# A graph layer's gather: 74 single rows per step instead of 40, in three list loads, with the list at partition 64

## The chip, the cores and the metric

The kernel runs on one core of one Trainium2 chip. The metric is the device time of one execution in microseconds. Before the change it is 15,322.12 us, the median of three runs (15,321.51 to 15,322.25).

## What is computed

One layer of a graph network with 50,000 nodes of 128 features and 1,650,000 edges, which are sorted by destination. Cut to what matters:

```python
Xs = X[src]
m_data = Xs @ W_data.T + b_data
m_ctrl = Xs @ W_control.T + b_control
msg = jnp.where((edge_types == 0)[:, None], m_data, m_ctrl)
agg = jax.ops.segment_sum(msg, dst, num_segments=X.shape[0])
x = _layernorm(x + relu(agg + (X @ W_self.T + b_self)))
```

For each edge the feature row of its source (512 bytes) has to be fetched, the rows are summed by destination and by edge type, and the sums go through the weights afterwards, since the products are linear.

## The kernel before

**Blocks and steps.** The sorted edges are cut into blocks, and a block into two steps (Q = 2). A step holds 12 chunks of 128 edges (R = 12), F = 42 fillers and S = 40 single rows, that is 1,618 edges; a block holds 3,236. The first block and the last hold chunks alone. This makes NBLK = 510 blocks.

**Three ways for an edge.** The rows of a chunk are fetched by one indirect DMA that POOL issues (`gathers`, L477): 128 rows into one column of a tile `y`, 24 such gathers per block, in four passes of six. There are ten tiles (SLOTS), so POOL may run some two and a half blocks ahead of the matmuls. The fillers take the place of edges in a chunk whose source is their own destination, since such rows need not be fetched; DVE puts them in (`fill`, L316 to L338). The single rows (`single_rows`, L437) go without POOL: SP and ACT issue one plain DMA of 512 bytes per row (L451), whose source address lies in a register. TURNS = (20, 20) says how many of a step's rows go by SP and by ACT.

**The list of single rows.** `load_edges` (L163) brings the row numbers of ten blocks into one partition (`one_g`); `offsets` (L430) has DVE multiply those of one block by 512 and write `at_x` (L435), 80 numbers in the order: SP's 40, then ACT's 40. Each queue reads its part of `at_x` into registers with a load (L446, TENSOR_LOAD in the profile), LOADS = 2 times per block, 20 numbers each, and issues 20 row fetches after each load. SP has another such load, L400, which reads the window starts of five blocks from the list `base_i`; DVE has one of one number per step, L509; and at the end each engine reads one number, L943.

**What PE does.** For each chunk a matmul (L496) with a one-hot matrix `oh` sums the rows by destination and type into `acc`. Once per step a further matmul (L502) adds the single rows. Ahead of it PE waits until all rows of the block have landed (`rows_fetched`, L456, wait at L460).

**What sets the order.** All is written out by hand, without a scheduler: each engine and queue runs its instructions in the order of the main loop (L614). In the turn of block b, the engines work like this:
- SP loads `xT` of block b+3 (L406), once in ten blocks the next group's edges, then the two parts of the single rows of block b+2, then stores the output of block b-1 (L563).
- ACT issues part 0 of the rows of block b+2, takes the square root for block b-1 (`root`, L551), which waits for DVE's moments (L546), and issues part 1.
- DVE finishes block b-1 (L541 to L546), builds the one-hot matrix and the counts of block b+2 (L412, L420), takes ACT's root (L557) and writes the output (L559), fills block b+5, and writes the row list of block b+3 (L435).
- A row tile `yx` has four buffers; the first fetch of a block waits until PE has used up the block four before.

Of the kernel before, what the change touches and what calls it, by code (L numbers as in the profile page):

```python
# [15 lines left out]
I32 = mybir.dt.int32  # L16
# [21 lines left out]
PASS = 6  # L38
B = 112
C = R * Q  # L40
F = 42
TURNS = (20, 20)
S = sum(TURNS)
LOADS = 2
X = Q * S
R1 = R + 1
C1 = Q * R1
# [2 lines left out]
CE = Q * SIZE  # L50
BE = CE + Q * F + X
NBLK = 2 + (E - CE) // BE
# [4 lines left out]
GB = 10  # L57
GROUPS = -(-NBLK // GB)
GC = GB * C1
AHEAD = 2  # L60
# [21 lines left out]
def plain(b):  # L82

    return b == 0 or b >= NBLK - 1
# [6 lines left out]
def straight(ctx, tc, c, x, x_t, src_t, dst_t, etype_t, src_f, dst_f, etype_f, src_x, dst_first, first_p, out):  # L91
# [17 lines left out]
    eds = ctx.enter_context(tc.tile_pool(name="eds", bufs=2))  # L109
# [3 lines left out]
    stp = ctx.enter_context(tc.tile_pool(name="stp", bufs=3))  # L113
# [13 lines left out]
                   allow_small_or_imprecise_dtypes=True)  # L127
    FILL = Q * F + C1
    small = keep_ps.tile([P, 2 * W + F + 2 * FILL + 2], F32, name="small")
    num_ps, rank_no_ps = small[:, :2 * W], small[:, 2 * W:2 * W + F]  # L130
    lists = [small[:, 2 * W + F + i * FILL:][:, :FILL] for i in range(2)]
    sums_at = [small[:Q * F, 2 * W + F + 2 * FILL + i:][:, :1] for i in range(2)]

# [27 lines left out]
    one_g = {}  # L161

    def load_edges(g):  # L163
        t = eds.tile([1, GB * X], I32, name="one_g")
        nc.sync.dma_start(t, src_x[None, g * GB * X:(g + 1) * GB * X])
        one_g[g] = t
        loads[g] = {}
        for name, a in (("s", src_t), ("d", dst_t), ("t", etype_t)):
            t = eds.tile([P, GB, C1], I32, name=name, bufs=1)
            nc.sync.dma_start(t.rearrange("p b c -> p (b c)"), a[:, g * GC:(g + 1) * GC])  # L170
            loads[g][name] = t
        for name, a in (("sf", src_f), ("df", dst_f), ("tf", etype_f)):
            t = eds.tile([GS, F], I32, name=name, bufs=1)
            nc.sync.dma_start(t, a[g * GS:(g + 1) * GS, :])
            loads[g][name] = t


    load_edges(0)
    BL = TBL
    first_i = keep.tile([P, BL, Q], I32, name="first_i")  # L180
# [211 lines left out]
    bys, pcs, zs, pls, bases, ats, ys = {}, {}, {}, {}, {}, {}, {}  # L392
# [23 lines left out]
    def counts(b):  # L416

        cnt = ohp.tile([P, Q, 2 * W], BF16, name="cnt")
        with nc.allow_low_precision(reason="whole numbers up to R1"):
            nc.vector.tensor_reduce(cnt, ohs[b].rearrange("p (q r) w -> p q w r", r=R1), AX.X, ALU.add)  # L420
        cnts[b] = cnt
# [8 lines left out]
    def offsets(b):  # L430

        if not plain(b):
            g, i = divmod(b, GB)
            ats[b] = stp.tile([1, X], I32, name="at_x", bufs=AHEAD + 2)
            nc.vector.tensor_scalar(ats[b], one_g[g][:, i * X:(i + 1) * X], float(ROW), None, op0=ALU.mult)  # L435

    def single_rows(b, part):  # L437

        if part == 0:
            ys[b] = stp.tile([S, Q, D], F32, name="yx", bufs=ROW_SLOTS)  # L440
        both = []
        for j, (eng, dma) in enumerate(((SP, nc.sync), (ACT, nc.scalar))):
            n = Q * TURNS[j]
            k0, k1 = part * n // LOADS, (part + 1) * n // LOADS
            at = Q * sum(TURNS[:j])
            _, rows = nc.values_load_multi_w_load_instructions(ats[b][0:1, at + k0:at + k1], engines=[eng], **RANGE)  # L446
            both.append([(dma, fetched[j][b % ROW_SLOTS], *divmod(k0 + k, TURNS[j]), sum(TURNS[:j]), row)
                         for k, row in enumerate(rows)])
        for pair in zip_longest(*both):
            for dma, sem, q, k, at, row in filter(None, pair):  # L450
                copy = dma.dma_start(ys[b][at + k:at + k + 1, q, :].bitcast(U8), x_bytes[:, bass.ds(row, ROW)])  # L451
                copy.then_inc(sem, 16)
                tc.no_tile_sem_insts.add(copy.ins.name)
                tc.add_to_no_dep_group(f"single{b}", copy.ins)

    def rows_fetched(b):  # L456

        times = len(range(b % ROW_SLOTS or ROW_SLOTS, b + 1, ROW_SLOTS))
        for j in range(2):
            wait = nc.tensor.wait_ge(fetched[j][b % ROW_SLOTS], 16 * Q * TURNS[j] * times)  # L460
        tc.declare_fence(wait.ins, group=f"single{b}")
# [132 lines left out]
    for b in range(1, AHEAD + 1):  # L594
        offsets(b)
# [7 lines left out]
    for b in range(1, RAHEAD):  # L603
# [3 lines left out]
        if b < AHEAD:  # L607
            onehot(b)
            counts(b)
            for part in range(LOADS):  # L610
                single_rows(b, part)
        if b == 1:
            clear_sums()
    for b in range(NBLK + 1):  # L614
# [5 lines left out]
        if i == 0 and g + 1 < GROUPS:  # L620
            load_edges(g + 1)
# [9 lines left out]
        for q, (step, ks) in enumerate(passes_of(b)):  # L631
# [26 lines left out]
            if q == 3:  # L658
                left_out_matrix(b + RAHEAD)
                offsets(b + AHEAD + 1)  # L660
            if q < LOADS and not plain(b + AHEAD):
                single_rows(b + AHEAD, q)
# [338 lines left out]
```

## Time and profile before

| what | value |
|---|---|
| runs | 15,321.51 to 15,322.25 us, median 15,322.12 |
| profiled execution | 15,323.45 us, its span 15,321.7 us |
| mean granted TensorE clock | 0.535 |
| DMA | mean 61 GB/s, 939.07 MB in 649,293 packets |
| share of 16 DMA engines: POOL's queue q0, q1, ACT's queue q10 | 20.9%, 2.9%, 0.3% |
| instructions | 197,234 |

The profile's first part gives each engine's busy time. Issuing a DMA, loading a register and waiting are not counted as busy there, so a queue that only issues looks idle; its instructions are seen in the views by source line, which give the number, the least, median and largest duration in ns, and the first and last start in us. A line of the waits names who waited, for whom, the sum in us, how often, and the longest; "issue" means that the engine waited for nothing that the profile shows. A line of the costliest groups ends with the busy time in us, the mean of one in ns, and the idle time just before them.

### The profile page before, as it was taken

Reading aid. Unit: us, or ns where it says so; the run is one execution under the profiler, and the core shown is the slowest. Engines: PE = TensorE matmul, PEld = TensorE weight load, DVE = VectorE, ACT = ScalarE, POOL = GpSimd, SP = SyncE. Lnnn points to the kernel's source line nnn. Section 1 sums busy time; section 2 is a strip of 40 time slices with the busy share of each in tenths; the row PEclk is TensorE's granted clock in tenths of the full one; section 3 lists DMA queues with packets and bytes.
Section 4 is the critical chain, followed back from the end, with each engine's and each line's share of the span. In section 5 each row is a group of like instructions: output and inputs, shape, how many; then the busy total and the mean of one; then the engine's idle time right before and its main releaser. Section 6 shows DMA issues by size and latency. Waiting matters only on the chain. (4 is left out here: it accounts for less than half of the span.)

```text
span 15321.7 us, 197234 instructions
## 1 busy us (share of the span) xinstructions
PE 8296.6 (54%) x35844; PEld 7096.5 (46%) x35845; DVE 10904.6 (71%) x13994; ACT 153.6 (1%) x516; POOL 11565.0 (75%) x12250
## 2 busy tenths in 40 slices
PE   3555555555555555555555555555555555555555
PEld 3444444444444444444444444444444444444444
DVE  8777777777777777777777777777777777777775
ACT  0000000000000000000000000000000000000000
POOL 7777777777777777777777777777777777777777
PEclk7555555555555555555555555555555555555555
DMA  2222222222222222222222222222222222222222
GB/s 65 62 61 62 61 62 61 62 62 61 62 61 62 61 62 61 62 61 62 62 60 62 61 62 61 62 62 61 61 62 62 61 62 61 62 61 62 62 61 56
DMA packets 649293, 939.07 MB, mean 61 GB/s; under 512 B 327756, under 2 KB 445487, under 8 KB 648034
## 3 DMA queue, kind: packets, MB, share of 16 engines
q0 software_dynamic: 391680, 802.93, 20.9%
q1 hardware_dynamic: 215276, 112.76, 2.9%
q10 hardware_dynamic: 41078, 10.68, 0.3%
q14 instruction: 968, 7.93, 0.2%
q8 instruction: 291, 4.77, 0.1%
HBM read 895.92 MB, written 29.42 MB: 60 GB/s over the span
## 5 line engine op out<-in xcount | busy, mean ns | idle before, releaser
L477 POOL DMA_INDIRECT y<-in_x,idx x12216 | 11540.9, 945 | 3733.3 <-issue 3552.2
L496 PE MATMUL acc<-oh,y 128*128 128x120 f32 x24480 | 5867.6, 429 | 5768.3 <-PEq L484 5767.8
L496 PEld LDWEIGHTS acc<-oh,y 128*128 128x128 f32 x24480 | 5313.7, 326 | 6190.7 <-PEq L484 6178.3
L420 DVE TENSOR_REDUCE cnt<-oh 128x240 bf16<-128x3120 f32 x510 | 2959.6, 5803 | 0.1
L541 DVE COPY h<-po 112x128 f32<-112x128 f32 x510 | 148.7, 292 | 2499.1 <-PE po L535 2407.5
L412 DVE TENSOR_TENSOR oh<-col,small 128x3120 f32<-128x3120 f32 x510 | 1719.5, 3372 | 0.0
L512 DVE TENSOR_TENSOR sums<-acc,sums 128x180 f32 x1020 | 352.2, 345 | 1393.1 <-PE acc L505 1236.0
L338 DVE TENSOR_REDUCE by<-old 128x84 bf16<-128x1092 f32 x508 | 1078.5, 2123 | 17.6
L502 PE MATMUL acc<-oh,yx 40*128 40x120 f32 x2032 | 777.4, 484 | 0.0
L345 PE MATMUL small<-ones_b,by 128*84 128x1 bf16 x508 | 117.4, 231 | 1191.1 <-DVE by L338 1191.1
L319 DVE TENSOR_TENSOR m<-rk,small 128x1092 f32<-128x1092 f32 x508 | 656.4, 1292 | 17.3
L322 DVE TENSOR_TENSOR new<-m,small 128x1092 f32<-128x1092 f32 x508 | 656.2, 1292 | 17.3
L326 DVE TENSOR_REDUCE v_new<-new 128x26 f32<-128x1092 f32 x508 | 655.8, 1291 | 17.3
L345 PEld LDWEIGHTS <-by 128*84 128x84 bf16 x508 | 74.3, 146 | 1267.3 <-DVE by L338 1267.2
L335 DVE TENSOR_TENSOR old<-m,small 128x1092 f32<-128x1092 f32 x508 | 652.3, 1284 | 0.0
L502 PEld LDWEIGHTS acc<-oh,yx 40*128 40x128 f32 x2032 | 497.5, 304 | 210.0 <-issue 205.3
L535 PE MATMUL po<-wmsgT,sums 128*112 128x128 f32 x2040 | 515.1, 396 | 0.0
L535 PEld LDWEIGHTS po<-wmsgT,sums 128*112 128x112 f32 x2040 | 374.0, 253 | 108.2 <-issue 88.7
L533 PE MATMUL po<-bias,sums 3*112 3x128 f32 x1020 | 350.3, 439 | 0.0
L525 DVE TENSOR_TENSOR sums<-pl,sums 128x336 f32<-128x336 f32 x508 | 257.9, 508 | 85.2 <-DVE sums L512 84.6
L532 PE MATMUL po<-wselfT,xT 128*112 128x128 f32 x1020 | 315.5, 412 | 0.0
L551 ACT ACTIVATE sd<-mv,eps 112x1 f32<-112x1 f32 x510 | 150.4, 295 | 15051.3 <-DVE mv L546 8335.5
(118 smaller groups left out, 4174.2 us busy)
## 6 DMA issues: line engine op xcount, KB each, us to landing
yx<-in_x ACTq DMA_DIRECT2D x20320, 0.5 KB
yx<-in_x SPq DMA_DIRECT2D x20320, 0.5 KB
y<-in_x,idx POOLq DMA_INDIRECT x12216
xT<-in_x_t SPq DMA_DIRECT2D x510, 56.0 KB
out<-o SPq DMA_DIRECT2D x510, 56.0 KB
vf_all<-vd SPq DMA_DIRECT2D x51, 420.0 KB
s<-in_src_t SPq DMA_DIRECT2D x51, 130.0 KB
d<-in_dst_t SPq DMA_DIRECT2D x51, 130.0 KB
```

The source lines that it names most:

```text
L319: nc.vector.tensor_tensor(m, rk_g[g][:, i, :, None].to_broadcast([P, C1, F]), rank_no_ps[:, None, :].to_broadcast([P, C1, F]), op=ALU.is_e ...
L322: nc.vector.tensor_tensor(new.rearrange("p (q r) f -> p q r f", r=R1), m.rearrange("p (q r) f -> p q r f", r=R1), vf.rearrange("p (q f) -> ...
L326: nc.vector.tensor_reduce(v, new, AX.X, ALU.add)
L335: nc.vector.tensor_tensor(old, m, cb[:, :, None].to_broadcast([P, C1, F]), op=ALU.mult)
L338: nc.vector.tensor_reduce(by, old.rearrange("p (q r) f -> p q f r", r=R1), AX.X, ALU.add)
L412: nc.vector.tensor_tensor(oh, col_g[g][:, i, :, None].to_broadcast([P, C1, 2 * W]), num_ps[:, None, :].to_broadcast([P, C1, 2 * W]), op=AL ...
L420: nc.vector.tensor_reduce(cnt, ohs[b].rearrange("p (q r) w -> p q w r", r=R1), AX.X, ALU.add)
L477: copy = nc.gpsimd.indirect_dma_start(out=y[:r, k % PASS, :].bitcast(U8), out_offset=None, in_=x_rows, in_offset=bass.IndirectOffsetOnAxis ...
L496: nc.tensor.matmul(acc[:, :2, :].rearrange("p t w -> p (t w)"), y[:r, k % PASS, :], ohs[b][:r, column(k), :], start=k == of_step[0], stop= ...
L502: nc.tensor.matmul(acc[:, :2, :].rearrange("p t w -> p (t w)"), ys[b][:, q, :], ohs[b][:S, q * R1 + R, :], start=False, stop=True)
L512: nc.vector.tensor_tensor(part, accs.pop((b, q)), part, op=ALU.add)
L535: nc.tensor.matmul(po, a[:, t, :B], c["wmsgT"][:, t * D:(t + 1) * D], start=False, stop=t == 1)
```

## The change

Of each step 74 edges become single rows instead of 40, 36 of them SP's and 38 ACT's. A queue reads its list in three loads per block instead of two, and issues a third part of rows in the third pass of the main loop (`q < LOADS`). There are 43 fillers instead of 42. The parts are cut by `part * n // LOADS`: SP's 72 rows of a block into 24, 24, 24, at positions 0, 24 and 48 of the block's list, and ACT's 76 into 25, 25, 26, at positions 72, 97 and 122. The lists `one_g` and `at_x` become tiles of 65 partitions of which the last one alone is used, so that they lie at partition 64 instead of 0; in the bytes of a partition they take 148 numbers per block instead of 80.

```diff
-F = 42
-TURNS = (20, 20)
+F = 43
+TURNS = (36, 38)
 S = sum(TURNS)
-LOADS = 2
+LOADS = 3
+AT = 64
 X = Q * S
...
     def load_edges(g):
-        t = eds.tile([1, GB * X], I32, name="one_g")
+        t = eds.tile([AT + 1, GB * X], I32, name="one_g")[AT:, :]
         nc.sync.dma_start(t, src_x[None, g * GB * X:(g + 1) * GB * X])
...
             g, i = divmod(b, GB)
-            ats[b] = stp.tile([1, X], I32, name="at_x", bufs=AHEAD + 2)
+            ats[b] = stp.tile([AT + 1, X], I32, name="at_x", bufs=AHEAD + 2)[AT:, :]
             nc.vector.tensor_scalar(ats[b], one_g[g][:, i * X:(i + 1) * X], float(ROW), None, op0=ALU.mult)
```

The lines of the new kernel are numbered one higher from here on (L477 is L478 there).

## The prediction

> **What bounds the kernel now.** I read the page first for the busiest engine, then the waits of that engine, then the two queues that the change loads, SP and ACT. These are lines of the page: the busy shares, the costliest group, and the two kinds of row fetch among the DMA issues.
>
> ```profile
> PE 8296.6 (54%) x35844; PEld 7096.5 (46%) x35845; DVE 10904.6 (71%) x13994; ACT 153.6 (1%) x516; POOL 11565.0 (75%) x12250
> ...
> L477 POOL DMA_INDIRECT y<-in_x,idx x12216 | 11540.9, 945 | 3733.3 <-issue 3552.2
> ...
> yx<-in_x ACTq DMA_DIRECT2D x20320, 0.5 KB
> yx<-in_x SPq DMA_DIRECT2D x20320, 0.5 KB
> y<-in_x,idx POOLq DMA_INDIRECT x12216
> ```
>
> The waits of POOL over the whole span:
>
> ```profile
> POOL y L477 <- issue: 3559.2, 11667, 0.3
> POOL y L477 <- DVE h L542: 74.9, 245, 0.3
> ```
>
> POOL looks only 75% busy, but it is the bound: its idle time is 0.3 us behind each gather, "issue", with nothing to wait for. Start to start the 12,240 gathers (12,216 and 24 of the last block) lie 1,250 ns apart in the mean (median 1,249, 99% under 1,267). 12,240 x 1.2503 = 15,304 us of the 15,321.7 us span; the 18 us left are the start and the last block's tail. A block of 24 gathers takes 30.0 us, and every other engine and queue has room as long as it needs less than 30.0 us per block. DVE needs 10,904.6 / 510 = 21.4 us, PE 16.3 us.
>
> ACT is "1% busy", but issuing is not counted as busy. These views are the list loads and row fetches by source line, L446 over the whole span and L451 in one part of a block:
>
> ```profile
> L446 ACTq TENSOR_LOAD <-at_x x1016: 1411/1437/1689, 16.8 to 15202.4; - x170
> L446 SPq TENSOR_LOAD <-at_x x1016: 1197/1378/1676, 26.8 to 15191.8; - x170
> ```
>
> ```profile
> L451 ACTq DMA_DIRECT2D yx<-in_x x20: 227/228/461, 8028.1 to 8034.4; - x20
> ```
>
> A load of 20 row numbers takes 1.44 us on ACT, and 20 rows are issued from 8028.1 to 8034.4. Averaged over all parts, a part on ACT is the load, 0.16 us, a first row that takes 0.56 us until the second, 0.326 us for each later row, and 0.24 us for the last one's own issue: 8.3 us for 20 rows. Two parts, the square root and gaps are 16.7 us per block. So ACT has 13 us of room per block; SP, with 16.2 us of rows and some 1.9 us of other issues, has 12.
>
> **The change, part by part.**
>
> *Blocks and gathers (removed).* A step holds 1536 + 43 + 74 edges instead of 1536 + 42 + 40, a block 3,306 instead of 3,236. So there are 500 blocks, not 510, and the last has 5 gathers, not 24: 499 x 24 + 5 = 11,981 gathers, 259 fewer. If POOL stays the bound: 259 x 1.2503 = -324 us, 14,998 us of span. That is the most that the change can give.
>
> *Row issues (added).* Per block SP issues 72 rows instead of 40 and ACT 76, in parts of 24, 24, 24 and 25, 25, 26. ACT without its loads: 0.16 + 0.56 + 23 x 0.326 + 0.24 = 8.46 us for a part of 25, 8.79 for 26, together 25.7 us, and 0.24 us for the square root and gaps: 25.9 us of the 30.0. Rows from both queues go out side by side in the trace already, at 227 to 228 ns, so I add nothing for that.
>
> *List loads (added, the disputed price).* What is left for three loads on ACT is 30.0 - 25.9 = 4.1 us. Their price hangs on where they start. The trace has another load, L400, which takes 5 values each time from one list, at positions 0, 5, 10 and so on. Here are two of them, at 518.8 us (position 20) and at 668.6 us (position 25), and the loads of one value at the end:
>
> ```profile
> L400 SPq TENSOR_LOAD <-base_i x1: 746/746/746, 518.8 to 518.8; - x1
> ```
>
> ```profile
> L400 SPq TENSOR_LOAD <-base_i x1: 1329/1329/1329, 668.6 to 668.6; - x1
> ```
>
> ```profile
> L943 ACTq TENSOR_LOAD <-bad x1: 465/465/465, 15314.7 to 15314.7; - x1
> L943 DVEq TENSOR_LOAD <-bad x1: 308/308/308, 15315.2 to 15315.2; - x1
> L943 SPq TENSOR_LOAD <-bad x1: 473/473/473, 15316.0 to 15316.0; - x1
> ```
>
> All 26 loads that start at a multiple of 4 take 714 to 840 ns, the 76 others 1,260 to 1,386, for the same 5 values. Five reads of one value each fit the 76: 473 + 4 x 204 = 1,290. One read of four and one of one fit the 26. The 20 values of L446 start at positions 0, 20, 40 and 60, all multiples of 4: five reads, (1,437 - 465) / 4 = 243 ns for each further one on ACT, 226 on SP. So I read it thus: from a multiple of 4 on, values come four at a time; from elsewhere, one at a time. Position 15, three past a multiple, would show it if one value came singly and the rest as four: it took 1,315 ns, so it doesn't.
>
> After the change ACT's list begins at position 72 and its parts at 72, 97 and 122. The first is a multiple of 4, the other two are not. SP's parts (0, 24, 48) all are; the built program puts each list on a 16-byte boundary. ACT's reads: 25 values as 6 fours and a one, 1.44 + 2 x 0.243 = 1.92 us; 25 values singly, 0.465 + 24 s; 26 values singly, 0.465 + 25 s. s is 204 ns by SP's L400 and 243 by ACT's reads of four; I take 219, SP's single read raised as ACT's reads of four stand to SP's (243 / 226). That gives 1.92 + 5.72 + 5.94 = 13.6 us (12.9 at 204, 14.8 at 243) where 4.1 are free.
>
> One rule is to be weighed here. The Trainium skill, "Runtime: NRT & Kernel Launch", Instruction fetch mechanics, has a register load cost some 200 ns per register even in bulk. The trace has 72 ns per value in the loads of 20 and contradicts it there, and agrees in the 76 dear loads of five. By the rule ACT would need 15.2 us for loads, an estimate, and the run 20.5 ms.
>
> *Sum.* ACT needs 25.9 + 13.6 = 39.5 us per block and becomes the bound. Nothing slows it further: its list for the next block comes from DVE some 10 us after the square root that ACT itself issues between its first and second part, so DVE's answer is there 19 us early. ACT's steady work begins with block 3, at 103.5 us in the trace (blocks 1 and 2 fit before, 2 x 39.5 us from 16.8 us on), and covers 496 blocks up to 498; behind its last row lie the landing, half a block of matmuls and the last layer, some 30 us (from the last gather to the end it is 16 us now). 104 + 496 x 39.5 + 30 = 19,730 us; with unrounded terms 19,740.
>
> *SP.* 28.8 us for three parts of 24 (8.03 to 8.10 us each now, plus 4 rows and one read of four), 0.5 for xT, 0.55 for the store, 0.25 for L400 shared by five blocks, 0.4 for the group's loads, 0.2 gaps: 30.7 us. It hides behind ACT's 39.5, but not behind POOL's 30.0.
>
> *The rest, at nothing.* 43 fillers lengthen five DVE operations of 7.3 us per block by 26 / 1092, 0.17 us, and at_x from 0.18 us to about 0.25: DVE goes to 21.7 us and hides behind ACT; without cover it would cost 0.25 x 500 = 120 us. The matmul of L502 contracts 74 rows instead of 40; L496 with 128 rows takes 429 ns, L502 with 40 takes 484, so rows cost nothing. The fetches take 0.3% (ACT's queue) of the DMA engines now. Partition 64 is the one thing without a row: a load there can't be cheaper than the cheapest load shown, 0.3 us, and I know no row that makes it dearer than at 0, so the bounds are 0.3 us for each load and 243 ns for each read; I take no effect. DVE's load of one value at partition 0 (L509) has a median of 304 ns amid all traffic, and 308 at the end with the queues empty: no sign that partition 0 is crowded. The Trainium skill, "SBUF — State Buffer", Door 1, says that partitions 64 apart are served by different DMA ports, which speaks for the move; no row here shows a gain from it.
>
> **Rivals.**
> 1. *The end of the run is faster.* A read at partition 64 costs less than a third, so three loads fit into 4.1 us (at most some 60 ns per read instead of 219). Then SP's loads fall too, from 4.9 us below 2, POOL stays the bound, and the span is 14,998 us: 15,000. For it: nothing shows a read there. Against: the 304 and 308 ns above.
> 2. *Only the values up to the next multiple of 4 come singly*, so parts 2 and 3 take 10 and 8 reads: 2.65 and 2.17 us. ACT needs 32.7 us, 16,340 us. If position cost nothing at all: 1.92 + 1.92 + 2.17, 31.9 us, 15,980. Still slower, since three loads and 76 rows don't fit into 30.0. Against: position 15.
> 3. *ACT's loads just fit, and SP sets the pace* with 30.7 us: 134 + 496 x 30.7 = 15,360, no change.
> That the change doesn't do what it says is excluded: the built program has 500 blocks, 11,981 gathers, and three loads of 24 to 26 numbers per queue and block.
>
> **How the numbers follow.** The profiled execution took 15,323.45 us for a span of 15,321.7 us; the runs' median is 15,322.12, 1.3 us less, so the sum stands for both. What a measurement here can tell from no change is 0.2%. Forecast (singly read loads bind ACT): 0.80, 19,740 us, by itself 19,380 to 20,320. Rival 2: 0.07. Rival 1: 0.10. Rival 3: 0.03. The range runs from rival 2's 16,300, which also covers reads that are somewhat cheaper at partition 64, to 20,900, for reads that are some 5% dearer than the dearest row: 0.95 of the forecast and most of rival 2. Faster 0.10, same 0.03, slower 0.87.
>
> **What would show it.** Loads of ACT near 1.9, 5.7 and 5.9 us in turn, of SP near 1.6; ACT's rows without a gap from block to block; POOL's idle time put down to PE instead of issue, and PE waiting for the fetched rows (L461 in the new numbering). Loads of under 2 us at all three positions would prove me wrong in the position rule, loads of about 1 us in the partition.

## The result, and the profile after

The kernel with the change takes 19,693.32 us (median of four runs, 19,582.59 to 19,800.39) where the kernel before takes 15,321.83: the ratio is 1.285, with a 95% interval from 1.275 to 1.295. The profiled execution took 19,582.59 us, with a span of 19,580.9. The four runs lie in two pairs 1.1% apart (19,583 and 19,587; 19,800 twice), for which no run shows a cause, and the working below is held against the lower pair, where the profile and all four runs of the same kernel in experiment e5 lie (19,578 to 19,586).

Busy time, the chain of work that ended last, by engine and then by line, POOL's group, and the matmul L503, ahead of which PE waits for the fetched rows, from the page of the kernel after:

```profile
PE 5715.8 (29%) x35101; PEld 5373.9 (27%) x35102; DVE 10810.8 (55%) x13719; ACT 150.5 (1%) x506; POOL 11310.9 (58%) x11991
...
ACTq 85%; issue 13%; ACT 1%; DVE 1%; PE 0%; DMA 0%; SPq 0%; DVEq 0%
ACTq L452 52%; ACTq L447 33%; ACT sd L552 1%; DVE cnt L421 0%; PE acc L497 0%; DVE by L339 0%; ACTq L552 0%; DVE new L323 0%; DVE m L320 0%; DVE v_new L327 0%; DVE old L336 0%; DVE oh L413 0%; PE po L536 0%; DMA first_i<-in_dst_first 0%; PE po L534 0%
...
L478 POOL DMA_INDIRECT y<-in_x,idx x11976 | 11304.8, 944 | 8194.6 <-PE acc L497 4449.5
...
L503 PE MATMUL acc<-oh,yx 74*128 74x120 f32 x1992 | 457.2, 318 | 0.0
```

Every busy share has fallen, and ACT still shows 1%, because issuing is not counted as busy. The chain tells what the shares hide: 85% of the span is ACT's own queue, 52% the row fetches of L452 and 33% the list loads of L447. A third of the span goes into reading numbers out of a list. POOL does 11,976 gathers instead of 12,216, at the same duration (944 ns, before 945), but now sits idle for 8,195 us of the span.

The list loads by source line, over the whole span and then on ACT alone in one block (8000 to 8042 us; duration in ns as least/median/most):

```profile
L447 ACTq TENSOR_LOAD <-at_x x1494: 1889/5598/6038, 16.9 to 19540.5; - x187
L447 SPq TENSOR_LOAD <-at_x x1494: 1578/1677/1903, 27.1 to 19509.0; - x187
```

```profile
L447 ACTq TENSOR_LOAD <-at_x x4: 1997/5570/5858, 7999.3 to 8038.3; - x4
```

SP's loads of 24 values take 1.68 us. ACT's of 25 and 26 have a median of 5.6 us, and a least of 1.9: the three parts are three different loads. Sorted by part, their medians are 1.997 us at position 72, 5.598 at 97 and 5.842 at 122. The first reads as many values as the second and takes a third of the time.

Who waits for whom, from the waits of the whole span (total us, times, longest us):

```profile
PEld L346 <- DVE by L339: 12746.6, 498, 30.3
...
DVE rstd L558 <- ACT sd L552: 6678.0, 498, 25.2
POOL y L478 <- PE acc L497: 4449.5, 646, 11.0
POOL y L478 <- issue: 3332.9, 10915, 0.3
...
POOL y L478 <- PEq L461: 27.5, 90, 0.3
```

Read it from effect to cause: POOL (third line) waits for PE to give its buffers back, PE's weight load (first line) waits for DVE, DVE (second line) waits for ACT's square root in 498 blocks, up to 25.2 us, and the root stands in ACT's queue behind rows and loads. The last line is POOL's, 27.5 us. PE itself stood idle for 0.0 us ahead of L503 (first fence), so it hardly ever waited at L461 for fetched rows.

ACT's timeline in that block (start us, us, what):

```profile
8004.96 33.20 ACTq L452 DMA_DIRECT2D yx<-in_x  x76
8038.26 0.29 ACT L552 ACTIVATE sd<-mv,eps 112x1 f32<-112x1 f32 x1 [38.72 <-issue]
```

76 rows with two loads between them fill 33.2 us, the third load comes behind the root at 8038.3, and there is no gap. From block to block ACT's period is 39.22 us in the mean. SP, which has 24 us of rows and 5 us of loads, waits 4,438.6 us in the span for its next list from DVE: it is not what limits.

### The profile page after: what moved, and what is told of

Its sections match the earlier page's. It is cut to its first block, busy times and chain, and to the rows that moved or that the text cites. A ratio compares the mean times of both kernels' runs of the same rounds, so it can differ in the third digit from the quotient of the medians.

```text
span 19580.9 us, 261977 instructions
## 1 busy us (share of the span) xinstructions
PE 5715.8 (29%) x35101; PEld 5373.9 (27%) x35102; DVE 10810.8 (55%) x13719; ACT 150.5 (1%) x506; POOL 11310.9 (58%) x11991
## 3 DMA queue, kind: packets, MB, share of 16 engines
q0 software_dynamic: 383392, 785.90, 14.3%
## 4 chain that ended last, share of the span: by engine, by line
ACTq 85%; issue 13%; ACT 1%; DVE 1%; PE 0%; DMA 0%; SPq 0%; DVEq 0%
ACTq L452 52%; ACTq L447 33%; ACT sd L552 1%; DVE cnt L421 0%; PE acc L497 0%; DVE by L339 0%; ACTq L552 0%; DVE new L323 0%; DVE m L320 0%; DVE v_new L327 0%; DVE old L336 0%; DVE oh L413 0%; PE po L536 0%; DMA first_i<-in_dst_first 0%; PE po L534 0%
## 5 line engine op out<-in xcount | busy, mean ns | idle before, releaser
L478 POOL DMA_INDIRECT y<-in_x,idx x11976 | 11304.8, 944 | 8194.6 <-PE acc L497 4449.5
L497 PE MATMUL acc<-oh,y 128*128 128x120 f32 x23962 | 4166.1, 345 | 0.1
L497 PEld LDWEIGHTS acc<-oh,y 128*128 128x128 f32 x23962 | 3925.1, 255 | 0.3
L339 DVE TENSOR_REDUCE by<-old 128x86 bf16<-128x1118 f32 x498 | 1078.3, 2165 | 17.2
L323 DVE TENSOR_TENSOR new<-m,small 128x1118 f32<-128x1118 f32 x498 | 657.5, 1320 | 17.0
L320 DVE TENSOR_TENSOR m<-rk,small 128x1118 f32<-128x1118 f32 x498 | 657.4, 1320 | 16.9
L327 DVE TENSOR_REDUCE v_new<-new 128x26 f32<-128x1118 f32 x498 | 656.3, 1318 | 17.0
L336 DVE TENSOR_TENSOR old<-m,small 128x1118 f32<-128x1118 f32 x498 | 653.8, 1313 | 0.0
L503 PE MATMUL acc<-oh,yx 74*128 74x120 f32 x1992 | 457.2, 318 | 0.0
L503 PEld LDWEIGHTS acc<-oh,yx 74*128 74x128 f32 x1992 | 380.6, 237 | 0.0
```

What stands on the lines that cost most here:

```text
L320: nc.vector.tensor_tensor(m, rk_g[g][:, i, :, None].to_broadcast([P, C1, F]), rank_no_ps[:, None, :].to_broadcast([P, C1, F]), op=ALU.is_e ...
L323: nc.vector.tensor_tensor(new.rearrange("p (q r) f -> p q r f", r=R1), m.rearrange("p (q r) f -> p q r f", r=R1), vf.rearrange("p (q f) -> ...
L327: nc.vector.tensor_reduce(v, new, AX.X, ALU.add)
L339: nc.vector.tensor_reduce(by, old.rearrange("p (q r) f -> p q f r", r=R1), AX.X, ALU.add)
L478: copy = nc.gpsimd.indirect_dma_start(out=y[:r, k % PASS, :].bitcast(U8), out_offset=None, in_=x_rows, in_offset=bass.IndirectOffsetOnAxis ...
L497: nc.tensor.matmul(acc[:, :2, :].rearrange("p t w -> p (t w)"), y[:r, k % PASS, :], ohs[b][:r, column(k), :], start=k == of_step[0], stop= ...
```

## Experiments

**Theory**: a list load that starts at a multiple of four values (16 bytes) reads four at a time; from any other position it reads one at a time, at 0.21 us each. Two of ACT's three parts start elsewhere, ACT becomes the bound, and that is the loss. **Rivals**: the partition (64) sets the price of a read; or only the first values up to the next multiple of four come singly; or the positions don't matter for the time, because more rows lose anyhow. The runs were made in four groups, each on one chip with runs of the kernel before beside them.

One fact has to be known to read them. On the chips of two groups (e1 to e4, and e9 to e11) the kernel before takes 19,301.02 and 19,232.97 us instead of 15,322. There, instructions of SP and ACT stall while both issue rows at once; the last section has the numbers. In these groups SP or ACT is the bound in every kernel that was profiled (in e3, which is the kernel before but for the partition, SP waits for 0.2 ms of 19.3), so their times are compared only inside a group, and what I take from them are durations of loads. The groups of e5 to e8 and of e12 have 15,324.96 and 15,321.62 us for before.

### e1_fours and e6_fours_again: the same rows, cut at multiples of four

Against the kernel after. SP's parts stay 24, 24, 24; ACT's become 24, 24 and 28, at positions 72, 96 and 120.

```diff
-            k0, k1 = part * n // LOADS, (part + 1) * n // LOADS
+            k0, k1 = (p * n // LOADS // 4 * 4 for p in (part, part + 1))
```

> The changed kernel with the parts of the lists cut at multiples of four: ACT reads 24, 24 and 28 numbers from positions 72, 96 and 120 instead of 25, 25 and 26 from 72, 97 and 122; SP's parts stay. Theory (a load that starts off a multiple of four reads its numbers one by one): ACT's loads fall to about 1.75, 1.75 and 1.95 us, ACT needs 25.9 + 5.5 = 31.4 us per block and is still the bound, 134 + 496 x 31.4 = 15,700 us. Rival (76 rows and three loads are too many wherever they start) and rival (loads at partition 64 are dear): ACT's loads stay as they are, 19,600 to 19,800 us.

Measured in the first group: 25,691.69 us, 1.330 [1.3237, 1.3364] of before. ACT's loads fell to some 1.7, 1.7 and 2.0 us, as the theory says, but the time says nothing. SP's timeline in this run:

```profile
8000.36 9.06 SPq L452 DMA_DIRECT2D yx<-in_x  x11
```

Eleven rows take 9.06 us here; over the whole run a row takes SP 0.63 us in the mean instead of 0.33, so SP needs 51.3 us per block and no longer lets ACT's loads show. Inconclusive; the same kernel was run again in the second group.

> The changed kernel with the parts cut at multiples of four (ACT 24, 24, 28). Theory (single reads off a multiple of four made ACT the bound): where rows take 0.32 us, ACT's loads are 1.7, 1.7 and 2.0 us, ACT needs 25.9 + 5.4 = 31.3 us per block and SP 30.7: 134 + 496 x 31.3 = 15,700 us, that is 4.0 ms less than the changed kernel and still 2% more than before. Rival (76 rows and three loads cost as much wherever they start): 19,600 us.

Measured: 16,068.54 us, 1.0485 [1.0471, 1.0500] of before, beside 19,579.01 for the kernel after on the same chip (e5). The loads of e6:

```profile
L447 ACTq TENSOR_LOAD <-at_x x1494: 1647/1765/2243, 17.0 to 16014.8; - x187
L447 SPq TENSOR_LOAD <-at_x x1494: 1579/1677/1903, 27.4 to 16031.0; - x187
```

No load above 2.3 us is left. Nothing but the places of two cuts differs, and it is worth 19,579.01 - 16,068.54 = 3,510 us of the 4,254 us that the change costs on this chip. That refutes the rival in which the positions don't matter. It is still slower than before, and 370 us above the 15,700 that I expected. The chain, by engine and by line, and the largest waits of SP in e6 show where to look:

```profile
SPq 33%; DVE 21%; DMA 16%; issue 13%; ACTq 11%; PE 6%; DVEq 0%; ACT 0%; PEldq 0%
SPq L452 26%; DMA yx<-in_x 16%; ACTq L452 9%; SPq L447 6%; DVE cnt L421 5%; PE acc L497 3%; DVE by L339 3%; ACTq L447 2%; DVE new L323 2%; DVE m L320 2%; DVE v_new L327 2%; DVE old L336 2%; PE acc L503 1%; PE po L536 1%; PE po L534 1%
```

```profile
SPq L175 <- DMA out<-o: 514.2, 48, 12.3
SPq L447 <- DVE mv L547: 73.7, 80, 1.7
```

SP heads the chain now. Its block takes 30.69 us in the median, more than POOL's 30.0; but the mean is 32.1, because once in ten blocks, where a group's lists are loaded, it takes 46 us: L175 waits 514.2 / 48 = 10.7 us there. This is such a place:

```profile
3288.37 0.34 SPq L564 DMA_DIRECT2D out<-o  x1
...
3292.50 0.34 SPq L175 DMA_DIRECT2D df<-in_dst_f  x1
3302.97 0.28 SPq L175 DMA_DIRECT2D tf<-in_edge_type_f  x1
```

The load of tf stands still from 3292.8 to 3303.0 until a store issued at 3288.4 has landed, 14.6 us after its issue. The store is late because it queues behind rows: in the trace's packet records a row's packet begins 8.3 us after its issue here (median), 0.7 us in the kernel before and 0.64 in the kernel after, where the same rows are spread over 39 us. The store itself shows it: 105 of its 112 packets begin within 2 us of its issue, the last seven at 3300.8 us, behind rows of SP that begin one after another until then. In 475 stores of this run it is seven each time, one sixteenth, in the median 9.0 us after the issue. That would fit if the rows of a queue all went through one of the 16 DMA engines, but the records don't name the engine. The chain's "DMA yx<-in_x 16%" is time between the issue of a row and its landing.

The wait need not be all of it. Through the six blocks that lead up to such a wait, the delay of ACT's rows grows from 4.7 to 11.1 us, 1.0 us per block. So in these blocks, in which SP doesn't wait, SP and ACT issue their rows faster than the queues take them up. No run takes away the wait alone; how the last 700 us divide between the two stays open.

### e2_partition0 and e10_partition0_again: the lists back at partition 0

Against the kernel after.

```diff
-AT = 64
+AT = 0
```

> The changed kernel with the lists back at partition 0, all else as changed. Theory (position in the list decides, not the partition): loads of 2.0, 5.6 and 5.8 us on ACT as at partition 64, 19,600 to 19,800 us, the same as the changed kernel. Rival (partition 64 makes the loads dear): loads of under 2.2 us and some 15,900 us.

> The changed kernel with its lists at partition 0, where rows are issued in 0.32 us. Theory (the partition has no effect): 19,580 us, the same as the changed kernel. Rival (partition 64 makes each read dearer): ACT's loads fall below 5 us and the time with them.

Measured: 26,122.65 us, 1.3525 [1.3461, 1.3590], and 26,025.93 us, 1.3547 [1.3523, 1.3571]. Both fell on chips that stall, so the times expected were missed and the kernel has no time on another chip. The loads are answer enough. Those of e10:

```profile
L447 ACTq TENSOR_LOAD <-at_x x1494: 822/5547/6097, 16.6 to 26039.4; - x187
L447 SPq TENSOR_LOAD <-at_x x1494: 3/1675/1927, 27.4 to 26007.0; - x187
```

By part, ACT's medians are 1.99, 5.55 and 5.85 us at partition 0, and 1.997, 5.598 and 5.842 at 64.

### e3_64_alone: partition 64 without the rest

Against the kernel before; its 40 rows and two loads are kept.

```diff
-        t = eds.tile([1, GB * X], I32, name="one_g")
+        t = eds.tile([AT + 1, GB * X], I32, name="one_g")[AT:, :]
...
-            ats[b] = stp.tile([1, X], I32, name="at_x", bufs=AHEAD + 2)
+            ats[b] = stp.tile([AT + 1, X], I32, name="at_x", bufs=AHEAD + 2)[AT:, :]
```

> The kernel before with the lists at partition 64 and nothing else. Theory: loads of 20 numbers take 1.44 us on ACT and 1.2 to 1.46 on SP as at partition 0, and POOL stays the bound: 15,322 us, no change. Rival (partition 64 makes loads dear): loads of 4 us or more; ACT and SP have 12 us of room, so the time would hide it and only the loads tell.

Measured: 19,330.95 us beside 19,301.02, 1.001 [0.9989, 1.0031]; ACT's loads have a median of 1.427 us (1.437 at partition 0). Some records of loads are far shorter on this chip, down to 3 ns, so e10's three parts are the firmer evidence on the loads. The partition does nothing, in the loads or in the time. The second of these is shown for a chip where SP and ACT are the bound, and so loads would count.

### e4_shift3: before, with its lists three values further on

Against the kernel before. All four parts begin three past a multiple of four.

```diff
-            ats[b] = stp.tile([1, X], I32, name="at_x", bufs=AHEAD + 2)
+            ats[b] = stp.tile([1, X + 4], I32, name="at_x", bufs=AHEAD + 2)[:, 3:X + 3]
```

> The kernel before with the list of each block three positions further on in its tile, so that every load starts three past a multiple of four (3, 23, 43, 63); nothing else. Theory (all numbers one by one): 0.465 + 19 x 0.215 = 4.55 us per load on ACT, 0.473 + 19 x 0.204 = 4.35 us on SP; ACT needs 16.7 + 6.2 = 22.9 us per block, below POOL's 30.0, so 15,322 us, no change. Rival (only the numbers up to the next multiple of four singly): 8 reads, 2.2 us. Rival (position doesn't matter): 1.44 us. The time is the same under all; the loads tell.

Measured: 20,862.38 us, 1.0797 [1.0745, 1.0849]. The loads:

```profile
L446 ACTq TENSOR_LOAD <-at_x x1016: 982/4480/4732, 16.7 to 20757.2; - x170
L446 SPq TENSOR_LOAD <-at_x x1016: 1436/4248/4530, 28.0 to 20815.8; - x170
```

The same 20 values take 4.48 us instead of 1.44 on ACT and 4.25 instead of 1.38 on SP, though one single read would have brought them to a multiple of four. So the second rival falls: a load is read by fours or singly as a whole, from its first position. (4,480 - 465) / 19 = 211 ns for each further value. No change of the time was expected, since POOL would hide 6 us of loads; on this chip POOL is not the bound and the loads are not hidden. That is a miss of the time, from the chip and not from the loads.

### e5_after_again: the kernel after, unchanged

> The changed kernel once more, to be read beside the next three on one chip. Where SP and ACT issue a row in 0.32 us, as in the profiles of before and after: 19,600 to 19,800 us, 39.2 us per block on ACT, ratio to before 1.28. Where they stall for some 0.7 us on many instructions, as in the first four runs: some 26,000 us.

Measured: 19,579.01 us, 1.2777 [1.2759, 1.2795]; ACT's period is 39.21 us. It is the comparison for e6 to e8.

### e7_s70_fours, e8_s64_fours and e11_s66_fours: fewer rows, cut at multiples of four

Against the kernel of e6.

```diff
-TURNS = (36, 38)
+TURNS = (34, 36)      # e7
+TURNS = (32, 34)      # e11
+TURNS = (32, 32)      # e8, with LOADS = 2 instead of 3
```

> As the last, with 70 rows per step, 34 by SP and 36 by ACT: parts of 20, 24, 24 and 24, 24, 24, all from multiples of four; 501 blocks and 12,010 gathers. Theory: ACT needs 3 x (8.13 + 1.7) + 0.24 = 29.7 us per block, SP 27.3 + 1.9 = 29.2, both below POOL's 30.0, so POOL is the bound again: 12,010 x 1.2503 + 18 = 15,034 us, 1.9% less than before. If the lists that come late once in ten blocks can't be made up for with 0.3 us of room: up to 15,200. Rival (rows and loads are too many): above 15,322.

Measured: 36,437.17 us, 2.378 [2.374, 2.381]. It is not a time of the row fetches. With 70 rows one step has only 42 edges left for its 43 filler places, and the kernel then runs its general path (`general`, L830) behind the tiled one. I had not looked for that limit. The tiled part by itself ends near 15,380 us, at 30.7 us per block, so it is no faster than the kernel before, where I had expected 15,034 to 15,200. L175 waits for the store here too (527.9 us, 49 times), and ACT's rows begin 8.8 us after their issue (median): 70 rows are too many for the queues as well.

> As the last, with 64 rows per step, 32 by SP and 32 by ACT, in two loads of 32 from multiples of four; 503 blocks and 12,054 gathers. Theory: a load of 32 is 8 reads of four, 0.465 + 7 x 0.243 = 2.17 us; ACT needs 2 x (2.17 + 0.16 + 0.56 + 30 x 0.326 + 0.24) + 0.24 = 26.1 us, SP some 27, POOL is the bound with room: 12,054 x 1.2503 + 18 = 15,089 us, 1.5% less than before. Rival: above 15,322.

Measured: 15,109.83 us, 0.9860 [0.9846, 0.9874]: 1.4% faster than before. Its loads of 32 values, POOL's group and POOL's largest wait:

```profile
L447 ACTq TENSOR_LOAD <-at_x x1002: 2124/2153/2430, 16.3 to 15007.4; - x167
L447 SPq TENSOR_LOAD <-at_x x1002: 2024/2117/2332, 26.7 to 15003.8; - x167
```

```profile
L478 POOL DMA_INDIRECT y<-in_x,idx x12048 | 11392.3, 946 | 3683.8 <-issue 3535.7
```

```profile
POOL y L478 <- issue: 3537.5, 11589, 0.3
```

32 values take 2.15 us on ACT, eight reads of four, where 25 took 5.6. POOL is the bound again, with 0.3 us of "issue" behind each gather as in the kernel before, and the gathers that fell away are gained: with 64 rows a step, SP and ACT both stay under 30.0 us per block. In the packet records a row begins 1.2 us after its issue (median).

> 66 rows per step, 32 by SP and 34 by ACT, in three loads from multiples of four; 502 blocks and 12,040 gathers. Theory (POOL is the bound as long as ACT and SP stay below 30.0 us): SP 27.1 + 1.9 + 1.0 = 30.0, ACT 28.3, so between POOL's 12,040 x 1.2503 + 18 = 15,072 us and some 15,150. Rival (the row fetches themselves are at the end of what their DMA queues carry, since with 74 rows in fours they began 8 us after their issue): over 15,150 us with rows that begin several us late.

Measured: 23,664.55 us, 1.2313 [1.2288, 1.2338], on a chip that stalls. It doesn't answer where between 64 rows (e8) and 70 (e7) the queues begin to fill. What it shows is that more rows cost much on such a chip even where no load is read singly.

### e9_s64_shift1: e8 with its lists one value further on

Against the kernel of e8.

```diff
-            ats[b] = stp.tile([AT + 1, X], I32, name="at_x", bufs=AHEAD + 2)[AT:, :]
+            ats[b] = stp.tile([AT + 1, X + 4], I32, name="at_x", bufs=AHEAD + 2)[AT:, 1:X + 1]
```

> The kernel with 64 rows per step in two loads of 32 (15,110 us), with its list one position further on in its tile, so that every load starts one past a multiple of four; nothing else. Theory (all numbers one by one): 0.465 + 31 x 0.215 = 7.1 us per load on ACT instead of 2.16, 0.473 + 31 x 0.204 = 6.8 us on SP instead of 2.04 to 2.14; SP needs 28 + 9.4 = 37 to 38 us per block, ACT 36, so 18,500 to 19,100 us. Rival (the start doesn't matter and the changed kernel was slow for its rows alone): 15,110 us.

Measured: 26,502.65 us, 1.3799 [1.3775, 1.3823], on a chip that stalls, so its time doesn't stand beside e8's. The loads do:

```profile
L447 ACTq TENSOR_LOAD <-at_x x1002: 4097/7007/7367, 16.9 to 26334.3; - x167
L447 SPq TENSOR_LOAD <-at_x x1002: 4198/6651/6896, 28.6 to 26408.5; - x167
```

One value further on, 32 values take 7.01 us instead of 2.15.

### e12_half_gathers: e6 with half of each gather

Against the kernel of e6, to find what holds its rows up: the gathers' packets, or the rows' own queues. Half of each chunk's edges is left out of the sums.

```diff
-            r = REST_ROWS[k] if b == NBLK - 1 else SIZES[k % R]
+            r = min(REST_ROWS[k], 64) if b == NBLK - 1 else 64
```

The line stands in the gathers and in the products.

> The kernel with 74 rows and parts at multiples of four (16,069 us where rows take 0.32 us), with gathers and products of 64 rows instead of 128: the other half of each chunk is left out of the sums. The number of gathers, rows and loads stays. There the fetches began 8 us after their issue, and once in ten blocks SP waited some 10 us for a store to land behind them. Theory A (the gathers' packets hold up the rows): the rows begin within 1 us again, SP's wait goes and SP needs 31.0 us per block, 15,550 us. Theory B (the rows fill their own queues): rows as late as before, 16,050 us. On a chip where SP and ACT stall each other at 0.6 to 0.8 us per row: 25,600 us as with whole gathers if the stall has nothing to do with them, nearer to 16,000 if it has.

Measured: 16,040.64 us, 1.0469 [1.0448, 1.0490]. The wait of SP is as long as in e6:

```profile
SPq L175 <- DMA out<-o: 567.6, 48, 14.8
```

A row still begins 8.1 us after its issue, and the block takes 32.0 us. The gathers move half as much (785.90 MB on POOL's queue in e6, 393.34 here) and take up the DMA engines half as long (21.0% and 10.7%), and the rows are as late as before. So it isn't the time that the gathers' packets take; but their number is the same, 383,392, as each one only became smaller, and that the number matters is not excluded. That the rows fill their own two queues fits the runs (148 in 32 us are 8 us late, 140 in 30.7 us 8.8, 128 in 30 us 1.2), but it is argued. The seven late packets of each store point to one sixteenth of a queue; whether rows spread over more of it would begin sooner was not tried.

## Why the prediction was right

- **POOL the bound before, ACT after.** Right: the chain is 85% ACT's queue.
- **Blocks and gathers.** Right: 11,976 gathers and 5 of the last block, at 944 ns. The gain they would give is real: e8, with 186 gathers fewer (12,048 and 6, for 12,240), should gain 186 x 1.25 = 233 us by it and gains 215.
- **Rows on ACT, 25.9 us per block without loads.** 39.22 - 13.44 = 25.8.
- **Loads on ACT, 13.6 us.** 1.997 + 5.598 + 5.842 = 13.44. The position rule, read from a load of five values elsewhere in the program, held. The price of a further single read, 219 ns, was 214 (5,598 - 465, over 24) and 215 (5,842 - 465, over 25). The Trainium skill, "Runtime: NRT & Kernel Launch", Instruction fetch mechanics, has some 200 ns per register even in bulk, where it budgets the register loads that the runtime adds to a kernel. The loads here are the kernel's own, from lists in SBUF. The figure agrees with the loads read singly to 7%, and is three times that of the loads from a multiple of four (2,153 / 32 = 67 ns in e8).
- **The sum.** ACT's steady work begins at 104.5 us (103.5 predicted), and 26 us lie between its last row and the end (30 predicted): 104.5 + 496 x 39.22 + 26 = 19,584, where the span is 19,580.9. The prediction's unrounded block, (19,740 - 134) / 496 = 39.53 us, is 0.31 us too long, half in the rows and half in the loads; 496 times that is 154 of the 159 us between 19,740 and the span. The median of the four runs is 47 us below the prediction, because two of them are 1.1% longer than the profile; that nearness is chance.
- **SP, 30.7 us, hidden behind ACT.** Hidden it is, but the size was 1.4 us short of e6's mean of 32.1. That e6's median block, 30.69, meets it is chance: my 30.7 has 0.4 us for the group's loads, which the median block doesn't issue, so an ordinary block was set 0.4 us too low. The other 1.1 us is the wait of one of the group's loads for a store (10.7 us, once in ten blocks), which I had left out. In the kernel after neither costs anything, as ACT covers both. "No change" of rival 3, 15,360, was therefore 700 us too low: with aligned loads the same rows give 16,069.
- **Rows from both queues side by side, at nothing.** Right for their issue in the kernel after (0.325 us from row to row on ACT and 0.328 on SP, as before), wrong for their queues as soon as ACT no longer holds them back (e6), and wrong on chips that stall (e1).
- **Partition 64, no effect.** Right (e3, e10). The same runs refute rival 1.
- **Rival 2.** Refuted by e4 and e9. Its second price, 15,980 "if position cost nothing", is near e6's 16,069, but by ACT's 31.9 us; in e6 SP heads the chain.
- **What would show it.** Loads 1.9, 5.7, 5.9 and 1.6: right. POOL idle through PE: right. PE waiting at L461 for rows: wrong, 0.0 us of idle time ahead of L503. The prediction has the square root between ACT's first and second part, but asks only whether the next list of DVE comes in time behind it. It doesn't follow the root further: the root comes as late as the rows ahead of it, DVE stops for it (6,678 us in the span), and PE stops for DVE before it comes to the wait for rows. The pace is the same, ACT's, but the wait shows at the root.

## What to carry to other kernels

Where a register load reads several values, let each load start at a multiple of four values from where the list begins, with the list on a 16-byte boundary as here: cut the parts there, and begin each queue's list there. An equal split (25, 25, 26) cost 3.5 of the 4.3 ms here. Where a list of short fetches is spread over queues, work out each queue's issue time per block with its loads and its store, as busy shares do not show it, and leave it room: with 64 rows and two aligned loads instead of 74 and three the change gains 1.4%, while with 74 rows and aligned loads it loses 4.9%, as the rows come late, and behind them a store and the next group's loads. When one engine issues both fetches and a small operation that others wait for, look for the stall at the small operation.

## What the runs showed of the hardware that was not expected

On two chips of those used, SP's and ACT's instructions stall while both queues issue rows at once. The rows of e1 there, on each queue (ns as least/median/most):

```profile
L452 ACTq MOVE yx<-in_x x37848: 2/29/1422, 19.2 to 25542.8; - x200
...
L452 SPq DMA_DIRECT2D yx<-in_x x35856: 1/228/2084, 32.0 to 25602.2; - x200
```

A register move, 29 to 38 ns in the kernel after, takes up to 1,422 ns here and a fetch's issue up to 2,084, though the medians are the same. Most of the long ones take 600 to 800 ns, a few 1,300 to 1,500. From row to row that makes 0.63 us on SP and 0.50 on ACT in the mean of e1. In e10, SP's rows take 0.41 us while ACT is in a load and 0.73 otherwise, ACT's 0.32 us while SP is in one and 0.55 otherwise. The gathers keep their 945 ns and a row's packet begins 0.63 us after its issue (median), so these two are not held up. The kernel before takes 19.2 to 19.3 ms on these chips, and all its runs of a group agree within 0.9%, so it doesn't come with a single run. Whether it is the chip or the time at which it was used is open, as no chip was used in two groups, and the runs don't show the cause. Where such a chip is what the kernel runs on, the share of rows fetched singly is worth another look, and the ratio to the kernel before is another there (1.35 in e2 and e10, the kernel after but for the partition).
